# Query projection of a fused attention and feed-forward kernel: which sub-products are computed whole and which are split once more, and where two sets of token sums stand

## The chip, the cores and the metric

The kernel runs on one core of a Trainium2 chip, in one launch. The metric is the device time of that launch in microseconds (us), as the median of several runs. The engines are named as in the profile: PE (TensorE, matrix products), DVE (VectorE), ACT (ScalarE), POOL (GpSimd) and SP (SyncE, which here only issues DMAs). Each engine works through its own list of instructions in order; semaphores make one engine wait for another.

## What is computed

The reference is a cross-attention block followed by a gated feed-forward block, all in float32, on 8 sequences of 128 tokens with 512 features (1024 tokens in all), with 32 heads of 128. The lines of the attention:

```
x = _rmsnorm(hidden_states, ln_weight)
...
h_q = (x @ w_q.T).reshape(b, lq, H, DH)
h_k = (key_value_states @ w_k.T).reshape(b, lk, H, DH)
h_v = (key_value_states @ w_v.T).reshape(b, lk, H, DH)
score = jnp.einsum('bqhd,bkhd->bhqk', h_q, h_k)
score = score + position_bias[None]
...
attn = jnp.einsum('bhqk,bkhd->bqhd', score, h_v).reshape(b, lq, H * DH)
out = attn @ w_out.T
return hidden_states + out
```

The change touches the first product alone, the queries `h_q`: 1024 x 512 times 512 x 4096.

## The kernel before

**Groups.** The 32 heads are worked in 8 groups of 4 (`NG = 8`, `GH = 4`). The queries of all groups are computed first, in the loop of lines 800 to 842, and written to HBM (`store_queries`); the attention reads them back later. For group g the product is a 512 x 512 piece of the weights (`wq`) times the 512 x 1024 transposed tokens (`hT`), giving four tiles `heads[0..3]` of 128 x 1024, one for each head.

**Seven products for eight.** That product is cut into 2 x 2 blocks on each side and done by the Strassen-Winograd scheme with seven block products, numbered 1 to 7, in place of eight. It needs sums of blocks beforehand: four sums of weight blocks for each group (`combine_rows`, line 315, on POOL, 128x512 each), and four sums of token blocks once for all groups (`h_sums`). A product of the outer scheme can be computed in one of two ways:

- *whole* (`whole`, line 367): two halves of two PE matmuls with 512 columns each; ACT copies every half from PSUM to its place in `heads`.
- *split once more* by the same scheme (`inner`, line 383): seven inner products, of 128 x 256 columns each, in the order 2, 1, 5, 6, 3, 7, 4. Each inner step ends in a DVE addition that takes the PSUM bank into `heads`. Two banks alternate: inner products 2, 5 and 3 go into one, and 1, 6, 7 and 4 into the other, so a later step has to wait until DVE has taken the earlier one out of its bank. A split product needs, for each group, four 128x128 weight sums on POOL (`q_inner_rows`, line 723), and once for all groups four 128x256 sums of its token block (`inner_tokens`, line 470, four DVE instructions for each product number, all of whose inputs lie in SBUF; the third one overwrites a piece of `hT`, so the product's whole form can't be computed after it).

**Who does what.** Outer products 2, 3, 4 and 5 are always split, all four together (`inner_T`, called *quads* here): seven steps of four matmuls and three DVE additions. The quads of group g are not computed in group g but interleaved into group g+1 (the generator `quads`). Outer product 1 is whole in every group. Products 6 and 7 are whole in group 0 and single split products in groups 1 to 7 (`inner_T6` in the two banks of the pool `ps_mm`, `inner_T7` in the banks `sc` and `av` of the pool `ps`).

**Order.** During this phase all instructions of PE, DVE, ACT and POOL keep the order of the program (`InOrder`). For groups 1 to 7 it is written out by hand: first whole product 1, each half followed by one step of the quads of the group before, then line 832:

```
for k, n in enumerate((6, 6, 0, 6, 6, 0, 7, 6, 7, 6, 0, 6, 7, 7, 0, 7, 7, 0, 7)):
    next(streams[n])
    if g + 1 < NG and k in (2, 5, 8, 10):
        weigh_q(q_w[g + 1], k // 3)
    if g + 1 < NG and k == 10:
        rows_now = combine_rows(f"q{g + 1}", q_w.pop(g + 1))
```

where 0 is a step of the quads. `weigh_q` (line 707) multiplies a quarter of the next group's weights by the norm's weights, on ACT; `combine_rows` follows on POOL when all four quarters are done, and `q_inner_rows` of the next group after it.

**Token sums.** All of `inner_tokens` stands in group 0: line 819 for products 2 to 5 (16 instructions) at the third half of the whole products, line 825 for products 6 and 7 (8 instructions) at the last half. Their results lie in `q_sums` (lines 809 to 812), addressed by `q_place`.

**Room.** The 128x128 weight sums of a group lie in one of two sets of spare tiles (`row_space`, `q_rows`), groups of even and odd number by turns, taken from buffers that the attention uses later (tags `aT`, `pb`, `s4`, `p`, `pT`, `tt`). The first position bias `pb0` (line 843) is loaded into a buffer of tag `pb`.

Of the kernel before, what the change touches and what calls it, by code (L numbers as in the profile page):

```python
# [10 lines left out]
F32 = mybir.dt.float32  # L11
# [6 lines left out]
P = 128  # L18
BS = 32
# [15 lines left out]
class Later:  # L35
# [10 lines left out]
    def next(self, engine):  # L46
        if self.calls:
            op, args, kw = self.calls.pop(0)
            getattr(engine, op)(*args, **kw)
# [15 lines left out]
def xattn_ffn_kernel(  # L65
# [26 lines left out]
    NG = H // GH  # L92
# [6 lines left out]
    HW = GW // 2  # L99
    ADD, SUB = ALU.add, ALU.subtract  # L100
# [11 lines left out]
    work = pool("work", 2, side="right", reuse_waits="tile")  # L112
# [50 lines left out]
    for b in range(B):  # L163
        nc.sync.dma_start(x_in[b // 2][:, b % 2, :], x[b])

    vector, gpsimd, scalar, sync = (
        InOrder(tc, e) for e in (nc.vector, nc.gpsimd, nc.scalar, nc.sync)
    )
# [198 lines left out]
    def whole(name, product, part, count, pool=ps_mm, tag="mm"):  # L367

        m, places = {}, ((1, [(1, 1)]), (6, [(1, 2)]), (7, [(2, 2), (2, 1)]))
        for i, to in places[:count]:  # L370
            for t in range(2):
                if i == 1:
                    m[t] = pool.tile([P, 512], F32, tag=tag, name=f"mm_{name}_{t}")
                product(i, t, m[t], i == 1)
                for r, c in to:
                    scalar.copy(part(r, c, t), m[t])  # L376
                yield
# [5 lines left out]
    def inner(name, multiply, places, banks=None, fresh=False):  # L383


        one, two = banks or (
            [pl.tile([P, 2, HW], F32, tag="i", name=f"i{k}{h}_{name}") for h in range(2)]
            for k, pl in enumerate((ps_a, ps_b))
        )
        blocks = {1: (1, 1), 2: (1, 1), 3: (1, 2), 4: (2, 1), 5: (2, 2), 6: (1, 2), 7: (2, 2)}  # L390
        steps = [(i, *blocks[i]) for i in (2, 1, 5, 6, 3, 7, 4)]
        for i, r, c in steps:
            for m, (ns, place) in zip(two if i in (2, 5, 3) else one, places):
                for h, n in enumerate(ns):
                    multiply(n, i, m[:, h], i in (2, 1, 5) and h == 0)
                for to, *base, out in place(r, c, m, *((i in (2, 5, 6, 4),) if fresh else ())):
                    vector.tensor_tensor(to, *(base or [to]), out, ADD)  # L397
            yield True

    def multiply_T(a, b):  # L400
        def multiply(n, i, out, first):
            kv_tensor.matmul(out, a[n][i], b[n][i], start=first, stop=True, skip_group_check=True)  # L402

        return multiply
# [13 lines left out]
        places = ((2, 3), upper), ((4, 5), lower)  # L418
        return inner(name, multiply_T(a, b), places, fresh=fresh)

    def inner_T7(name, a, b, heads):
        def place(r, c, m, first):
            above, to = (heads[k][:, bass.ds(512 + (c - 1) * HW, HW)] for k in (r - 1, r + 1))
            return [(to, above if first else to, m[:, 0])]

        banks = [[ps.tile([P, 2, HW], F32, tag=tag, name=f"{tag}_{name}")] for tag in ("sc", "av")]
        return inner(name, multiply_T(a, b), (((7,), place),), banks, True)

    def inner_T6(name, a, b, heads):
        def place(r, c, m, first):  # L430
            left, to = (heads[r - 1][:, bass.ds(at + (c - 1) * HW, HW)] for at in (0, 512))
            return [(to, left if first else to, m[:, 0])]

        banks = [[ps_mm.tile([P, 2, HW], F32, tag="mm", name=f"m6{k}_{name}")] for k in range(2)]
        return inner(name, multiply_T(a, b), (((6,), place),), banks, True)

    def inner_V(name, a, b, pairs):
        def multiply(n, i, out, first):
# [31 lines left out]
    def inner_tokens(eng, src, half, place, products):  # L470

        blocks = {}
        for n in products:
            b = [src[n][:, c, at] for c in range(2) for at in (slice(0, half), slice(half, None))]
            b11, b12, b21, b22 = b
            t1, t2, t3, t4 = place(n)
            eng.tensor_tensor(t1, b12, b11, SUB)
            eng.tensor_tensor(t2, b22, t1, SUB)
            eng.tensor_tensor(t3, b22, b12, SUB)
            eng.tensor_tensor(t4, b21, t2, SUB)  # L480
            blocks[n] = numbered(*b, t1, t2, t3, t4)
        return blocks

    def blocks_T(name, w, src, heads):

        for j in range(GH):
            heads.append(acts.tile([P, T], F32, tag="a", name=f"{name}_{j}"))

        def product(i, t, out, first):
            for c in range(HC):  # L490
                kv_tensor.matmul(  # L491
                    out, w[i][:, c, bass.ts(t, P)], src[i][:, c, :],
                    start=(first and c == 0), stop=(c == HC - 1), skip_group_check=True,
                )

        def part(r, c, t):
            return heads[2 * (r - 1) + t][:, bass.ts(c - 1, 512)]

        return product, part
# [207 lines left out]
    def weigh_q(w, c):  # L707

        InOrder(tc, nc.scalar).mul(w[:, c], w[:, c], lnw_sb[:, c : c + 1])
# [3 lines left out]
    def spare(tag, bufs, shape=(2, 2, P)):  # L713
        return work.tile([P, *shape], F32, tag=tag, name=f"rows_{tag}", bufs=bufs)

    def row_space(tags, single):
        tiles = [spare(*t) for t in tags]
        sevens, sixes = (spare(*t, (3, P)) for t in single)
        return [t[:, k] for t in tiles for k in range(2)], {7: sevens, 6: sixes}

    q_rows = [row_space((("aT", 2), ("aT", 2), ("pb", 2)), (("s4", 1), ("p", 1)))]

    def q_inner_rows(g, w):

        pieces, single = q_rows[g % 2]
        a = {}
        for n in (6, 7) if g else ():
            quarters = [w[n][:, c, bass.ts(r, P)] for r in range(2) for c in range(2)]
            a[n] = sums_a(gpsimd, *quarters, *(single[n][:, k] for k in range(3)))
        a.update(pair_rows(w, pieces))  # L730
        return a
# [56 lines left out]
    def store_queries(g, heads):  # L788
        for j in range(GH):
            nc.sync.dma_start(queries[g][:, j, :], heads[j])  # L790
# [2 lines left out]
    kept = [dram.tile([P, 2, GW], F32, name=f"v0_kept_{i}") for i in range(B // 2)]  # L793

    def q_place(n):
        t1, t2, t4 = q_sums[3 * (n - 2) :][:3]
        return t1, t2, h_t[n][:, 0, slice(8, None)], t4

    quads, rows_now, h_inner = iter(()), rows_q, {}
    for g in range(NG):  # L800
        if g + 1 < NG:
            q_w[g + 1] = load_q(g + 1)
        else:
            kv_w[1] = load_kv(1)
        if g == 0:
            for i in range(B // 2):
                nc.sync.dma_start(kept[i], v[i])
            q_rows.append(row_space(3 * (("pT", 4),), 2 * (("tt", 2),)))
            q_sums = [
                acts.tile([P, 4, 8, BS], F32, tag="a", name=f"t_q{k}") for k in range(4)  # L810
            ] + [work.tile([P, 2, 8, BS], F32, tag="pT", name="t_q", bufs=4)]
            q_sums = [t[:, k] for t in q_sums for k in range(t.shape[1])]
        w, heads, name = rows_now, [], f"q{g}"
        tiles = whole(name, *blocks_T(name, w, h_t, heads), 1 if g else 3)
        a = q_inner_rows(g, w) if g else a_q0
        for k, _ in enumerate(tiles):
            next(quads, None)
            if g == 0 and k == 2:
                h_inner.update(inner_tokens(vector, h_t, 8, q_place, (2, 3, 4, 5)))
                vector.reciprocal(rs1, rs1)  # L820
                vector.tensor_scalar_add(res_scale, rs1, 1.0)
                vector.tensor_tensor(res_bias, mv1[:, :, 0], rs1, ALU.mult)
                vector.tensor_scalar_mul(res_bias, res_bias, -1.0)
            if g == 0 and k == 5:
                h_inner.update(inner_tokens(vector, h_t, 8, q_place, (6, 7)))
            if g == 0 and k >= 2:
                weigh_q(q_w[1], k - 2)
        if g:
            streams = {
                6: inner_T6(name, a, h_inner, heads), 7: inner_T7(name, a, h_inner, heads), 0: quads  # L830
            }
            for k, n in enumerate((6, 6, 0, 6, 6, 0, 7, 6, 7, 6, 0, 6, 7, 7, 0, 7, 7, 0, 7)):
                next(streams[n])
                if g + 1 < NG and k in (2, 5, 8, 10):
                    weigh_q(q_w[g + 1], k // 3)
                if g + 1 < NG and k == 10:
                    rows_now = combine_rows(f"q{g + 1}", q_w.pop(g + 1))
                if k == 17:
                    store_queries(g - 1, heads_before)
        if g == 0:  # L840
            rows_now = combine_rows("q1", q_w.pop(1))
        quads, heads_before = inner_T(name, a, h_inner, heads, g > 0), heads
# [719 lines left out]
```

## Time and profile before

| what | value |
|---|---|
| median of 3 runs | 1063.97 us (1063.6 to 1064.22) |
| the profiled execution: its own time | 1064.58 us |
| its span from first to last instruction | 1062.8 us |
| granted TensorE clock | 1.00 |
| POOL, DVE busy over the span | 535.3 us (50%), 751.8 us (71%) |
| query phase: first query matmul to the last | 55.4 to 230.2 us |
| group 1's first matmul | 65.7 us |
| groups 2, 3 begin | 88.20, 109.77 us |

The profile shows for each engine when it is busy. In the timeline a row is a run of equal instructions: start, length, engine, line, operation, output and inputs, shape, count, and in brackets the idle time before it and what ended it. Every float32 matmul appears as two records, so "x4" beside 128x512 is one half of a whole product (two matmuls), and "x8" beside 128x256 is one step of the quads (four matmuls); a single split step is "x2". In this phase most instructions carry line L60, which is the helper that records the order; they are told apart by their tiles: `mm_q` are banks of whole products, `m_q` banks of product 6, `sc_q` and `av_q` banks of product 7, `i_q` banks of the quads, `t_q` the token sums, `rows_...` and `S_q` the weight sums. Times are us from the start of the span.

### The profile page before, as it was taken

How to read it: one execution, taken by the hardware profiler on the slowest of the kernel's cores; microseconds unless marked ns; L12 is line 12 of the kernel's file. 1: busy time of each engine (PE TensorE's matmuls, PEld its weight loads, DVE VectorE, ACT ScalarE, POOL GpSimd, SP SyncE). 2: the span in 40 equal slices, each digit the busy share in tenths (PEclk: the TensorE clock that was granted, in tenths of full speed). 3: DMA queues.
4: the chain of work that ended last, by engine and by line, in shares of the span. 5: the costliest groups of instructions: out<-in, count | busy, mean ns of one | idle time of the engine just before them, and what ended most of it. 6: DMA issues, size and time to landing. Idle time of an engine off the chain costs nothing.

```text
span 1062.8 us, 14764 instructions
## 1 busy us (share of the span) xinstructions
PE 1052.6 (99%) x5156; PEld 845.8 (80%) x5156; DVE 751.8 (71%) x1415; ACT 305.3 (29%) x856; POOL 535.3 (50%) x583
## 2 busy tenths in 40 slices
PE   9999999999999999999999999999999999999998
PEld 5668878876888898888889769998888865667887
DVE  4697777798678778778777766774545237889852
ACT  2541112014544444444444333311000012333100
POOL 6648765808754656555552375570000336997010
PEclk9999999999999999999999999999999999999999
DMA  9543453396556554564656557774441632120011
GB/s 292 160 167 132 150 186 127 119 345 219 177 191 193 181 190 142 188 196 161 210 168 200 190 180 254 235 250 140 167 139 60 197 102 60 40 60 1 1 40 40
DMA packets 125850, 166.07 MB, mean 156 GB/s; under 512 B 15728, under 2 KB 77424, under 8 KB 125776
## 3 DMA queue, kind: packets, MB, share of 16 engines
q1 hardware_dynamic: 111360, 133.92, 38.2%
q10 hardware_dynamic: 12544, 24.38, 6.6%
q0 software_dynamic: 1872, 6.82, 2.0%
q8 instruction: 41, 0.67, 0.2%
q14 instruction: 33, 0.27, 0.1%
HBM read 106.90 MB, written 58.20 MB: 155 GB/s over the span
## 4 chain that ended last, share of the span: by engine, by line
PE 89%; DVE 5%; DMA 3%; issue 1%; ACT 1%; ACTq 0%; POOL 0%; SPq 0%; DVEq 0%; POOLq 0%
PE m L913 9%; PE i_q L60 9%; PE m L60 8%; PE mm_v L512 7%; PE mm_k L491 7%; PE i_v L440 7%; PE d L1468 6%; PE i L1333 6%; PE i_k L402 6%; PE mm_f L1373 5%; PE av L591 4%; PE sc L545 4%; PE mm_k L60 2%; PE m_q L60 2%; PE mm_q L60 2%; PE mm_v L60 2%
## 5 line engine op out<-in xcount | busy, mean ns | idle before, releaser
L60 DVE TENSOR_TENSOR q<-q,i_q 128x512 f32<-128x512 f32 x168 | 94.7, 596 | 30.9 <-PE i_q L60 27.8
L530 POOL TENSOR_TENSOR s<-pb,mneg 128x512 f32<-128x512 f32 x40 | 62.4, 1562 | 86.2 <-DVE p L569 78.0
L558 ACT ACTIVATE s<-s,nmx 128x128 f32<-128x128 f32 x240 | 93.3, 390 | 25.4 <-DVE nmx L553 18.7
L397 DVE TENSOR_TENSOR v<-v,i_v 128x512 f32<-128x512 f32 (+1 forms) x126 | 73.8, 589 | 34.7 <-PE i_v L440 23.1
L596 ACT COPY aT<-av 128x512 f32<-128x512 f32 x60 | 35.1, 585 | 168.4 <-PE av L591 130.8
L397 DVE TENSOR_TENSOR k<-k,i_k 128x512 f32<-128x512 f32 (+1 forms) x105 | 60.2, 588 | 27.6 <-PE i_k L402 26.9
L60 POOL TENSOR_TENSOR s<-pb,mneg 128x512 f32<-128x512 f32 x24 | 36.7, 1534 | 69.8 <-DVE p L60 39.0
L545 PEld LDWEIGHTS sc<-k,q 128*128 128x128 f32 x416 | 53.8, 192 | 6.6 <-issue 4.5
L545 PE MATMUL sc<-k,q 128*128 128x128 f32 x416 | 55.3, 275 | 0.0
L512 PE MATMUL mm_v<-wv,ctx_sb 128*128 128x256 f32 x224 | 52.5, 379 | 0.0
L491 PE MATMUL mm_k<-ctx_sb,wk 128*128 128x512 f32 x112 | 52.4, 593 | 0.0
L60 PE MATMUL m<-wo,a 128*128 128x256 f32 x200 | 48.5, 380 | 1.3 <-DMA a<-att 1.3
L301 DVE TENSOR_TENSOR S_a<-a 128x256 f32<-128x256 f32 x22 | 9.7, 443 | 56.3 <-DMA a<-att 43.2
L1108 POOL TENSOR_TENSOR x<-x,u 128x256 f32<-128x256 f32 x4 | 3.0, 753 | 91.8 <-DVE x L1107 91.8
L913 PE MATMUL m<-wo,a 128*128 128x256 f32 x200 | 48.4, 379 | 0.0
L591 PE MATMUL av<-pT,v 128*128 128x128 f32 x360 | 47.6, 275 | 0.0
L512 PEld LDWEIGHTS mm_v<-wv,ctx_sb 128*128 128x128 f32 x224 | 41.5, 190 | 5.0
L558 ACT ACTIVATION_READ_ACCUMULATOR s<-s,nmx 128x1 f32 x240 | 44.8, 187 | 0.0
L376 ACT COPY q<-mm_q 128x512 f32<-128x512 f32 x22 | 12.7, 586 | 110.7 <-PE mm_q L60 110.6
L569 DVE TENSOR_TENSOR p<-s,ri 128x512 f32<-128x512 f32 x52 | 43.3, 833 | 0.9
L591 PEld LDWEIGHTS av<-pT,v 128*128 128x128 f32 x360 | 43.8, 192 | 0.0
L60 PEld LDWEIGHTS m<-wo,a 128*128 128x128 f32 x200 | 37.2, 190 | 6.4 <-DMA a<-att 1.7
(433 smaller groups left out, 2742.7 us busy)
## 6 DMA issues: line engine op xcount, KB each, us to landing
queries<-q SPq DMA_DIRECT2D x32, 512.0 KB, 4.0
turned<-tt SPq DMA_DIRECT2D x64, 256.0 KB, 2.9
pT<-turned SPq DMA_DIRECT2D x64, 256.0 KB, 3.0
att<-aT ACTq DMA_DIRECT2D x64, 256.0 KB, 3.0
q<-queries SPq DMA_DIRECT2D x30, 512.0 KB, 5.1
a<-att SPq DMA_DIRECT2D x23, 512.0 KB, 4.0
wq<-in_wqT_dram SPq DMA_DIRECT2D x8, 1024.0 KB, 6.6
wk<-in_wkT_dram SPq DMA_DIRECT2D x7, 1024.0 KB, 5.6
```

The source lines that it names most:

```text
L60: return self.tc.keep_in_program_order(getattr(self.engine, op)(*args, **kw))
L397: vector.tensor_tensor(to, *(base or [to]), out, ADD)
L402: kv_tensor.matmul(out, a[n][i], b[n][i], start=first, stop=True, skip_group_check=True)
L440: kv_tensor.matmul(out[:, bass.ts(k, S)], b[n][i][:, bass.ts(k, S)], a[n][i], start=first and k == 0, stop=True, skip_group_check=True,)
L491: kv_tensor.matmul(out, w[i][:, c, bass.ts(t, P)], src[i][:, c, :], start=(first and c == 0), stop=(c == HC - 1), skip_group_check=True,)
L512: kv_tensor.matmul(out[:, bass.ts(k, HW)], src[i][:, c, bass.ts(2 * t + k, S)], w[i][:, c, :], start=(first and k == 0 and c == 0), stop=( ...
L545: tensor.matmul(sc[:, j, :], qT[:, j, bass.ts(b % 2, S)], kT[j][:, cols], start=True, stop=True)
L558: scalar.activation(s[:, j, :], s[:, j, :], AF.Exp, bias=nmx[:, j : j + 1], accum_out=sm[:, j : j + 1],)
L591: tensor.matmul(av[:, j, :], v[b // 2][:, b % 2, bass.ts(j, P)], pT[:, :, j, :], start=True, stop=True,)
L913: tensor.matmul(m[n], sa[n][:, c, :], wo_t[g][n][:, c, :], start=(g == order[0] and c == 0 and PRODUCTS.index(n) % 2 == 0), stop=(g == ord ...
L1333: nc.tensor.matmul(out, a[n][k], fine_t[n][k], start=first, stop=True, skip_group_check=True)
L1468: nc.tensor.matmul(out, lhs, rhs, start=bank not in started, stop=(i == NP - 1 or n == 8), skip_group_check=True,)
```

## The change

Three things change in the query phase.

- In groups 2 to 7 no product is whole: product 1 is split as well. Its inner steps that write a block for the first time are ACT copies (128x256), the others DVE additions. In group 1 products 1 and 6 are whole, and only 7 is a single split product. Group 0 stays as it was.
- The order is written anew: for group 1 (after the four halves of the whole products, each followed by a step of the quads) `7707707707`, for the later groups `1101160161061607676076707707`. The banks of single products now alternate between the pair in `ps_mm` and the pair `sc`, `av` from one product to the next. `weigh_q` and `combine_rows` hang on other places of the order, and `store_queries` of the group before follows after the whole order.
- The token sums of product 7 stay in group 0; those of 6 are issued in group 1 after the second step of the order, and those of 1 after the fifth. With product 1 split there are four token sums that were not there before, and four more 128x128 weight sums on POOL in each of groups 2 to 7; in group 1 four fewer. The tiles for them are taken from tags `s` and `pb`, so `pb0` is now loaded late in the query phase.

```diff
                 for to, *base, out in place(r, c, m, *((i in (2, 5, 6, 4),) if fresh else ())):
-                    vector.tensor_tensor(to, *(base or [to]), out, ADD)
+                    if base == [None]:
+                        scalar.copy(to, out)
+                    else:
+                        vector.tensor_tensor(to, *(base or [to]), out, ADD)
...
-    def inner_T7(name, a, b, heads):
...
-    def inner_T6(name, a, b, heads):
...
+    def inner_single(name, n, a, b, heads, banks):
+        def place(r, c, m, first):
+            cols = [bass.ds(at + (c - 1) * HW, HW) for at in (0, 512)]
+            corner, left = (heads[r - 1][:, at] for at in cols)
+            base, to = {
+                1: (None, corner), 6: (corner, left), 7: (left, heads[r + 1][:, cols[1]]),
+            }[n]
+            return [(to, *([base] if first else []), m[:, 0])]
+
+        return inner(f"{name}_{n}", multiply_T(a, b), (((n,), place),), banks, True)
...
-        for n in (6, 7) if g else ():
+        for n in ((), (7,), (1, 6, 7))[min(g, 2)]:
...
-        t1, t2, t4 = q_sums[3 * (n - 2) :][:3]
+        t1, t2, t4 = q_sums[3 * ((n - 2) % 7) :][:3]
...
+    ORDERS = [
+        [(int(n), k) for k, n in enumerate(order)]
+        for order in ("7707707707", "1101160161061607676076707707")
+    ]
+    bank_pairs = itertools.cycle([2 * [(ps_mm, "mm")], [(ps, "sc"), (ps, "av")]])
...
-            q_rows.append(row_space(3 * (("pT", 4),), 2 * (("tt", 2),)))
+            q_rows.append(row_space(3 * (("pT", 4),), 2 * (("tt", 2),) + (("s", 3),)))
+            q_rows[0][1][1] = spare("s", 3, (3, P))
             q_sums = [
                 acts.tile([P, 4, 8, BS], F32, tag="a", name=f"t_q{k}") for k in range(4)
-            ] + [work.tile([P, 2, 8, BS], F32, tag="pT", name="t_q", bufs=4)]
+            ] + [spare(tag, n, (2, 8, BS)) for tag, n in (("pT", 4), ("s", 3), ("pb", 2))]
...
-        tiles = whole(name, *blocks_T(name, w, h_t, heads), 1 if g else 3)
+        blocks = blocks_T(name, w, h_t, heads)
         a = q_inner_rows(g, w) if g else a_q0
-        for k, _ in enumerate(tiles):
+        for k, _ in enumerate(whole(name, *blocks, 3 - g) if g < 2 else ()):
             next(quads, None)
...
             if g == 0 and k == 5:
-                h_inner.update(inner_tokens(vector, h_t, 8, q_place, (6, 7)))
-            if g == 0 and k >= 2:
-                weigh_q(q_w[1], k - 2)
+                h_inner.update(inner_tokens(vector, h_t, 8, q_place, (7,)))
+            if k >= 2:
+                weigh_q(q_w[g + 1], k - 2)
         if g:
-            streams = {
-                6: inner_T6(name, a, h_inner, heads), 7: inner_T7(name, a, h_inner, heads), 0: quads
-            }
-            for k, n in enumerate((6, 6, 0, 6, 6, 0, 7, 6, 7, 6, 0, 6, 7, 7, 0, 7, 7, 0, 7)):
+            streams = {0: quads}
+            for n, order in ORDERS[g > 1]:
+                if n not in streams:
+                    pair = next(bank_pairs)
+                    banks = [
+                        [pl.tile([P, 2, HW], F32, tag=tag, name=f"{tag}_{name}_{n}")]
+                        for pl, tag in pair
+                    ]
+                    streams[n] = inner_single(name, n, a, h_inner, heads, banks)
                 next(streams[n])
-                if g + 1 < NG and k in (2, 5, 8, 10):
-                    weigh_q(q_w[g + 1], k // 3)
-                if g + 1 < NG and k == 10:
+                if g == 1 and order in (1, 4):
+                    h_inner.update(inner_tokens(vector, h_t, 8, q_place, (6 - 5 * (order // 4),)))
+                if g == 1 and order in (0, 3):
+                    weigh_q(q_w[2], 2 + order // 3)
+                if 1 < g < NG - 1 and order in (8, 11, 14, 17):
+                    weigh_q(q_w[g + 1], order // 3 - 2)
+                if g + 1 < NG and order == (18 if g > 1 else 4):
                     rows_now = combine_rows(f"q{g + 1}", q_w.pop(g + 1))
-                if k == 17:
-                    store_queries(g - 1, heads_before)
+            store_queries(g - 1, heads_before)
```

More of the change, by code (lines that the diff above doesn't have):

```diff
@@ L419, in inner_T @@
         return inner(name, multiply_T(a, b), places, fresh=fresh)
-    def inner_T7(name, a, b, heads):
+    def inner_single(name, n, a, b, heads, banks):
         def place(r, c, m, first):
[L423 to L427, printed above, removed]
-    def inner_T6(name, a, b, heads):
[L430 to L435, printed above, removed]
+            cols = [bass.ds(at + (c - 1) * HW, HW) for at in (0, 512)]
[5 more added lines that the diff above has]
+        return inner(f"{name}_{n}", multiply_T(a, b), (((n,), place),), banks, True)
     def inner_V(name, a, b, pairs):
@@ L717, in row_space @@
         tiles = [spare(*t) for t in tags]
-        sevens, sixes = (spare(*t, (3, P)) for t in single)
-        return [t[:, k] for t in tiles for k in range(2)], {7: sevens, 6: sixes}
+        singles = [spare(*t, (3, P)) for t in single]
+        return [t[:, k] for t in tiles for k in range(2)], dict(zip((7, 6, 1), singles))
     q_rows = [row_space((("aT", 2), ("aT", 2), ("pb", 2)), (("s4", 1), ("p", 1)))]
```

## The prediction

> **What bounds the kernel now.** First the page: how busy each engine is, and the chain that ended last.
>
> ```profile
> PE 1052.6 (99%) x5156; PEld 845.8 (80%) x5156; DVE 751.8 (71%) x1415; ACT 305.3 (29%) x856; POOL 535.3 (50%) x583
> PE 89%; DVE 5%; DMA 3%; issue 1%; ACT 1%; ACTq 0%; POOL 0%; SPq 0%; DVEq 0%; POOLq 0%
> ```
>
> PE is busy through 99% of the span: a matmul removed is a gain, a wait put before PE is a loss. Next the busy time by stretches (busy us and count for PE, PEld, DVE, ACT, POOL, then clock, DMA share, GB/s), around group 1 and in group 2:
>
> ```profile
> 72.00:92.00 20.00, 19.38 (x85) 15.72 (x84) 17.11 (x38) 2.73 (x5) 19.38 (x30) 1.00 0.26 101
> 92.00:110.00 18.00, 18.00 (x81) 15.21 (x80) 14.86 (x32) 3.15 (x5) 14.80 (x22) 1.00 0.34 124
> ```
>
> In group 1 POOL has no pause (19.38 of 20 us) and DVE little (17.11). That is the place to which the change moves work. The timeline of PE gives the unit prices:
>
> ```profile
> 75.95 1.19 PE L60 MATMUL m_q<-t_q,rows_tt 128*128 128x256 f32 x4 [0.62 <-DVE q L60]
> 87.77 0.59 PE L60 MATMUL sc_q<-t_q,wq 128*128 128x256 f32 x2
> 88.20 1.88 PE L60 MATMUL mm_q<-hT,wq 128*128 128x512 f32 x4
> 102.00 1.89 PE L60 MATMUL i_q<-hT,rows_pT 128*128 128x256 f32 x8
> 109.77 1.88 PE L60 MATMUL mm_q<-hT,wq 128*128 128x512 f32 x4
> ```
>
> Lengths overlap, so starts count: a single split step takes 87.77 to 88.20 = 0.43 us, a quads step (102.00 to 103.72) 1.73, half a whole product (88.20 to 89.92) 1.72. Groups 2 to 7 repeat every 109.77 - 88.20 = 21.57 us with no gap. Last the timelines of DVE and POOL, where token sums meet weight sums:
>
> ```profile
> 67.24 0.42 DVE L60 TENSOR_TENSOR t_q<-hT,t_q 128x256 f32<-128x256 f32 x1
> 68.03 1.38 DVE L60 TENSOR_TENSOR t_q<-hT,t_q 128x256 f32<-128x256 f32 x1
> 69.33 1.49 DVE L60 TENSOR_TENSOR hT<-hT 128x256 f32<-128x256 f32 x1
> 70.74 1.49 DVE L60 TENSOR_TENSOR t_q<-hT,t_q 128x256 f32<-128x256 f32 x1
> 78.43 1.61 DVE L60 TENSOR_TENSOR q<-q,i_q 128x512 f32<-128x512 f32 x3
> 80.29 0.41 DVE L60 TENSOR_TENSOR q<-q,m_q 128x256 f32<-128x256 f32 x1
> 80.62 0.42 DVE L60 TENSOR_TENSOR q<-q,sc_q 128x256 f32<-128x256 f32 x1
> 390.52 0.66 DVE L565 TENSOR_TENSOR ri<-sm,unseen 128x4 f32<-128x4 f32 x1
> ```
>
> ```profile
> 67.65 1.47 POOL L60 TENSOR_TENSOR S_q<-wq 128x512 f32<-128x512 f32 x1 [24.03 <-ACT wq L60]
> 69.20 1.33 POOL L60 TENSOR_TENSOR S_q<-S_q,wq 128x512 f32<-128x512 f32 x1
> 70.49 1.45 POOL L60 TENSOR_TENSOR wq<-wq 128x512 f32<-128x512 f32 x1
> 83.95 1.27 POOL L60 TENSOR_TENSOR S_q<-S_q,wq 128x512 f32<-128x512 f32 x1
> 390.39 0.76 POOL L304 TENSOR_TENSOR s_k<-S_k,s_k 128x256 f32<-128x256 f32 x1
> ```
>
> A token sum takes 0.34 us from start to start while POOL rests (66.90, 67.24, 67.58), but some 1.4 beside POOL's 128x512 sums, and each ends 0.29 us after the POOL instruction that was running (69.41 after 69.12, 70.82 after 70.53). The tiny `ri` at 390.52, also with two SBUF inputs, lasts 0.66 us and ends 0.03 after a 128x256 POOL sum; elsewhere it takes 0.15. DVE additions that read PSUM aren't affected: three for a quads step take 78.43 to 79.96 = 1.53, a single 0.33, POOL busy beside them.
>
> **Products exchanged.** A whole product costs 2 x 1.72 = 3.44 us, a single split one 7 x 0.4315 = 3.02 (0.4315 = 1.73 / 4). Groups 2 to 7: 28 + 21 matmuls x 0.4315 = 21.14 against 21.57, so -0.43 each, -2.6 together. Group 1 becomes 4 x 1.72 + 35 x 0.4315 = 22.0, 0.43 more than the pattern; but before it lasted 65.68 to 88.20 = 22.52, since it held a stall of about 0.9 (the row at 75.95 and its late matmuls), caused by the slow token sums of 67.6 to 72.2.
>
> **Cover in groups 2 to 7.** DVE: 7 x 1.53 + 17 x 0.33 = 16.3 us of 21.14; step by step every bank is out 0.4 us or more before PE wants it. POOL: 5.0 (four 128x512) + 3 x 1.78 + 5.7 = 16.1 of 21.14; the new sums of product 1 come first, some 17 us after group begin (weights weighed at 11.4, 5.0 of 128x512 sums, 0.5), and PE wants them at 21.14 + 2.6. ACT: a new copy of 128x256 has no row; it is bounded by 0 and the 0.58 of the 128x512 copy, I take 0.45. Three come early in the group while ACT idles. The fourth stands behind two `weigh_q` that wait for a DMA:
>
> ```profile
> 97.12 2.56 ACT L60 ACTIVATE wq<-wq,lnw_sb 128x512 f32<-128x512 f32 x4 [2.97 <-DMA wq<-in_wqT_dram]
> ```
>
> That is 8.9 us after group 2's begin; two of the four end at 10.2, the copy at 10.6, and product 7's second step, which takes over that bank, comes at 12.5. So 0, and as much as the DMA is later than 1.9 us if this cover goes. The late `pb0` (256 KB) arrives in group 7, some 25 us before the first scores at 233.6: 0. The stores, now behind the whole order, stand in SP's list where they stood, ahead of the next group's weights, and the tiles they free are wanted a group later: 0.
>
> **Token sums in group 1.** Unhindered, PE would run: products 1 and 6 and four quads steps, 65.68 to 79.46; then 7,7 to 80.33; quads 5 to 82.05; 7,7 to 82.92; quads 6 to 84.64; 7,7 to 85.51; quads 7 to 87.23; 7 to 87.66. DVE gets quads step 4 (begun 77.74) 1.06 us after its begin, ends it at 80.6 and two additions of 7 at 81.27; now its list has the sums of 6. POOL began at 67.65 and has done four 128x512 (5.0), four 128x128 (1.8) and eight 128x256 (5.7): it is at 80.2, waits until 80.4 for ACT, whose last three `weigh_q` now stand behind the copy of product 6 at 78.0, and starts group 2's four 128x512 sums, exactly then. The four token sums end with these, at about 86.2 (4.9 us). Queued behind: the three additions of quads step 5 (to 87.7) and two of product 7 (88.05, 88.4). PE's next step of 7 needs the first of those banks: it stands from 84.64 to 88.1, 3.5 us. Then the sums of 1, beside POOL's 128x128 sums. No row shows that pair; the bounds are 0.34 each (alone) and 1.41 (beside 128x512), and I take POOL's own 0.42 plus the 0.16 by which its 1.25 grows to 1.41: 0.58, since the 390.52 row waits out the shorter instruction and no more. 88.4 + 2.3 = 90.7. Only then quads step 6 leaves its bank, first half at 91.4; PE, ready at 89.0 for quads step 7, loses 2.4 more. Steps 7 and the last 7 end at 93.56: 5.4 us later than 88.20 before.
>
> [...]
>
> **Sum.** -2.6 + 5.4 = +2.8 us. On the profiled execution's own 1064.58 that is 1067.4; its span is 1062.8, the 1.8 around it stay. The median lies 0.61 below that execution: 1063.97 + 2.8 = **1066.8 us**. A measurement can tell 0.2%, 2.1 us: below 1061.8 is faster, above 1066.1 slower. With every token sum at 1.41 the second four take 5.6 instead of 2.3: +6.1, 1070.1.
>
> **Rivals.**
> (a) The sums cost what they do alone, 0.34, because POOL happens to wait then or DVE wins. DVE: sums of 6 to 82.6, step 5 and two to 84.8, sums of 1 to 86.2; quads 7 starts at 86.9, group 1 ends at 89.1: +0.9, with -2.6 is -1.7: 1062.3, no change that can be told. Against: POOL had 0.62 us of pause in 20.
> (b) Faster: the sums are hidden altogether. The stall before 76 us goes and DVE's additions of quads steps 5 and 6 leave the banks before PE returns: -2.6 - 0.54 (group 1: 87.66 against 88.20) = -3.1, 1060.9. It decides from the point where PE loses less than 1.0 us in all. For it: DVE has 5 us of spare time per group; against: after 79.46 it must do 3 x 1.53 + 7 x 0.33 = 6.9 us in PE's 8.2, before any sum.
> (c) Worse: the fourth ACT copy. If the weights land more than 1.9 us later than before, product 7 stands in each of groups 2 to 6; 1 us each makes +7.8, 1071.8. Against: landing came 7.9 to 8.9 us after group begin in all groups.
>
> **Chances.** Forecast 0.6, with its own range of 1065.5 to 1068.1, an error of one POOL sum (1.3 us) in where POOL stands; all sums at 1.41 0.05; (a) 0.17; (b) 0.13; (c) 0.05. Of the forecast's 0.6 some 0.13 lies below 1066.1. Slower 0.57, within 0.2% 0.30, faster 0.13. The range runs from just under (a) to all sums at 1.41, 1061.9 to 1070.1, and leaves out (b) and (c).
>
> **What would show it.** Right: in the changed profile the sums of 6 (`hT<-hT` and its three neighbours) near 81 to 86 us, 1.2 to 1.5 us each beside `S_q` on POOL; those of 1 near 0.6; two waits of PE on DVE of about 3.5 and 2.4 us; group 2 beginning near 93.6; then a period of 21.14 without gaps. Wrong: sums of 0.42, no wait of PE there, a period other than 21.14, or PE waiting for ACT at product 7.

## The result and the profile after

| | before | after |
|---|---|---|
| median | 1063.78 us (1063.56 to 1064.22, 4 runs) | 1069.05 us (1068.5 to 1070.21, 4 runs) |
| ratio to before, 95% interval | | 1.005 [1.0033, 1.0068] |
| the profiled execution: its own time, its span | 1064.58, 1062.8 us | 1069.48, 1067.7 us |
| group 2 begins; first matmul of the next phase (`mm_k`) | 88.20; 230.18 us | 95.63; 235.14 us |

The changed kernel is slower by about 5.3 us, as forecast in sign, and 2.25 us above the forecast of 1066.8. The page, its busy times and the shares of the chain that ended last:

```profile
PE 1053.9 (99%) x5186; PEld 853.5 (80%) x5186; DVE 759.9 (71%) x1430; ACT 308.3 (29%) x870; POOL 543.5 (51%) x603
PE 89%; DVE 5%; DMA 3%; ACT 1%; issue 1%; POOL 0%; ACTq 0%; SPq 0%; DVEq 0%; POOLq 0%
```

Read alone, this page misleads: PE is busy for 1.3 us more than before (1052.6) although the change takes work away from it in six groups (seven matmuls of 256 columns in place of four of 512, so the count of records rises by 30). The time by stretches says why. Its columns are busy us and count for PE, PEld, DVE, ACT and POOL, then the granted clock, DMA share and GB/s:

```profile
84.00:88.40 4.40, 1.02 (x5) 0.57 (x4) 4.40 (x7) 0.00 (x0) 4.32 (x7) 1.00 0.00 0
88.80:95.20 6.40, 5.34 (x13) 3.78 (x12) 4.78 (x10) 0.00 (x0) 6.24 (x11) 0.50 0.36 144
95.60:97.00 1.40, 1.40 (x8) 1.22 (x8) 1.21 (x4) 0.37 (x1) 1.32 (x3) 1.00 0.17 70
```

At the end of group 1 PE stands for most of 4.4 us; afterwards it is granted **half its clock**, from about 88.6 to 95.4 us, and matmuls that take twice as long count as busy. The timeline of PE, with the idle time before a row and what ended it in brackets (in this kernel the `mm_q` rows of 128x256 in group 1 are steps of product 7, and those of `av_q` and `mm_q` that begin groups 2 and 3 are steps of product 1):

```profile
84.43 0.59 PE L60 MATMUL i_q<-hT,S_q 128*128 128x256 f32 x2
88.43 1.04 PE L60 MATMUL mm_q<-hT,rows_tt 128*128 128x256 f32 x2 [3.40 <-DVE q L60]
91.39 1.22 PE L60 MATMUL i_q<-t_q,wq 128*128 128x256 f32 x2 [1.06 <-DVE q L60]
92.40 1.06 PE L60 MATMUL i_q<-t_q,S_q 128*128 128x256 f32 x2
93.25 1.06 PE L60 MATMUL i_q<-t_q,wq 128*128 128x256 f32 x2
95.63 0.59 PE L60 MATMUL av_q<-hT,wq 128*128 128x256 f32 x2
116.78 1.03 PE L60 MATMUL mm_q<-hT,wq 128*128 128x256 f32 x4
```

Both predicted waits are there, each for DVE: 3.40 and 1.06 us. The 128x256 rows behind the first one last 1.04 to 1.22 us in place of 0.59; from start to start it is 0.85 (92.40 to 93.25) in place of 0.43. Group 2 begins at 95.63, group 3 at 116.78: a period of 21.15. DVE and POOL in the same stretch:

```profile
81.67 0.54 DVE L60 TENSOR_TENSOR t_q<-hT 128x256 f32<-128x256 f32 x1
82.25 1.37 DVE L60 TENSOR_TENSOR t_q<-hT,t_q 128x256 f32<-128x256 f32 x1
83.54 1.48 DVE L60 TENSOR_TENSOR hT<-hT 128x256 f32<-128x256 f32 x1
84.95 1.48 DVE L60 TENSOR_TENSOR t_q<-hT,t_q 128x256 f32<-128x256 f32 x1
86.35 1.60 DVE L60 TENSOR_TENSOR q<-q,i_q 128x512 f32<-128x512 f32 x3
88.53 0.41 DVE L60 TENSOR_TENSOR rows_s<-hT 128x256 f32<-128x256 f32 x1
89.47 0.67 DVE L60 TENSOR_TENSOR hT<-hT 128x256 f32<-128x256 f32 x1
90.66 1.60 DVE L60 TENSOR_TENSOR q<-q,i_q 128x512 f32<-128x512 f32 x3
```

```profile
80.66 1.27 POOL L60 TENSOR_TENSOR S_q<-wq 128x512 f32<-128x512 f32 x1 [0.21 <-ACT wq L60]
83.30 1.44 POOL L60 TENSOR_TENSOR wq<-wq 128x512 f32<-128x512 f32 x1
84.71 1.44 POOL L60 TENSOR_TENSOR S_q<-wq,S_q 128x512 f32<-128x512 f32 x1
89.22 0.63 POOL L60 TENSOR_TENSOR S_q<-S_q 128x128 f32<-128x128 f32 x1
```

The four sums of product 6 take 81.67 to 86.35, 4.68 us, in step with POOL's 128x512 sums; the four of product 1 (the rows `rows_s<-hT` and `hT<-hT`; their results lie in spare tiles with the names of weight sums) take 88.53 to 90.66, 2.13 us, and POOL's 128x128 sums beside them last 0.63 in place of 0.45.

### The profile page after: what moved, and what is told of

The parts are those of the page before. It is cut to its first block, busy times and chain, and to the rows that moved or that the text cites. A ratio compares the mean times of both kernels' runs of the same rounds, so it can differ in the third digit from the quotient of the medians.

```text
span 1067.7 us, 14878 instructions
## 1 busy us (share of the span) xinstructions
PE 1053.9 (99%) x5186; PEld 853.5 (80%) x5186; DVE 759.9 (71%) x1430; ACT 308.3 (29%) x870; POOL 543.5 (51%) x603
## 4 chain that ended last, share of the span: by engine, by line
PE 89%; DVE 5%; DMA 3%; ACT 1%; issue 1%; POOL 0%; ACTq 0%; SPq 0%; DVEq 0%; POOLq 0%
PE m L925 9%; PE i_q L60 9%; PE m L60 7%; PE mm_v L510 7%; PE mm_k L489 7%; PE i_v L438 7%; PE d L1480 6%; PE i L1345 6%; PE i_k L405 6%; PE mm_f L1385 5%; PE mm_q L60 4%; PE av L589 4%; PE sc L543 4%; PE mm_k L60 2%; PE mm_v L60 2%; PE sc_q L60 1%
## 5 line engine op out<-in xcount | busy, mean ns | idle before, releaser
L547 DVE TENSOR_TENSOR s<-sc,s 128x512 f32<-128x512 f32 x52 | 35.3, 680 | 9.4 <-PE sc L543 9.4
```

## The experiments

All were timed in five rounds beside the kernel before (medians 1063.64 in the first set of four, 1063.70 in the second set of three). The diffs are against the changed kernel.

**1. No sums of 6 and 1.** Are the token sums the whole loss? The kernel leaves them out: without an engine `inner_tokens` issues nothing, and POOL fills their tiles with zeros early.

```diff
-                    h_inner.update(inner_tokens(vector, h_t, 8, q_place, (6 - 5 * (order // 4),)))
+                    h_inner.update(inner_tokens(None, h_t, 8, q_place, (6 - 5 * (order // 4),)))
...
+            for k in (12, 13, 14, 18, 19, 20):
+                gpsimd.memset(q_sums[k], 0.0)
```

> The changed kernel without the eight token sums of products 6 and 1 (they are left out of the computation; their tiles are zeroed early by POOL, while it rests). Theory: the whole loss hangs on these sums, so PE has no wait in group 1, group 2 begins 22.0 us after group 1 (29.7 in the changed kernel), the clock stays at 1.00, and the time is about 3.1 us below the kernel before, near 1060.7 us. Rival, that something else of the change costs time (the new banks, the ACT copies, the other order): PE still waits in groups 1 to 7, and the time stays above 1063.

Measured: 1061.04 us (1059.73 to 1061.97, 11 runs), ratio 0.9975 [0.9966, 0.9983]. The timeline of PE has no wait in this phase, and group 2 begins 7.86 us earlier than in the changed kernel:

```profile
87.77 0.59 PE L60 MATMUL av_q<-hT,wq 128*128 128x256 f32 x2
```

All of the loss hangs on the eight sums; without them the change brings 2.6 us.

**2. POOL rests beside the sums.** The order of DVE stays, but POOL, before it starts group 2's weight sums, reads one column of the last result of product 1's sums.

```diff
+                if g == 1 and order == 4:
+                    rest = small.tile([P, 1], F32, tag="rest", name="rest", bufs=1)
+                    gpsimd.tensor_scalar_add(rest, q_sums[20][:, 0, :1], 0.0)
```

> All eight sums in place on DVE, but a tiny POOL instruction that reads the last of them stands ahead of group 2's weight sums, so POOL rests while DVE does them. Theory, that the sums are slow because they wait out POOL's instructions: each takes 0.34 us from start to start, PE waits once, about 1.4 us, in group 1 and perhaps 0.4 us for POOL's late sums in group 2, and the time is about 1.5 us below the kernel before, near 1062.3. Rival, that eight more DVE instructions in a row are too much whatever POOL does: the waits of 3.4 and 1.1 us stay and the time is near 1069.

Measured: 1063.79 us (1062.71 to 1065.93, 11 runs), ratio 1.0005 [0.9996, 1.0014]. The timelines of DVE and of PE:

```profile
82.28 0.43 DVE L60 TENSOR_TENSOR t_q<-hT,t_q 128x256 f32<-128x256 f32 x1
82.62 0.42 DVE L60 TENSOR_TENSOR hT<-hT 128x256 f32<-128x256 f32 x1
```

```profile
85.38 0.67 PE L60 MATMUL mm_q<-hT,rows_tt 128*128 128x256 f32 x2 [0.20 <-DVE q L60]
87.69 0.70 PE L60 MATMUL i_q<-t_q,wq 128*128 128x256 f32 x2 [1.20 <-DVE q L60]
90.02 0.59 PE L60 MATMUL av_q<-hT,wq 128*128 128x256 f32 x2
```

The sums start 0.34 us apart, 0.42 each, on the same engine behind the same instructions: POOL's sums beside them are what made them 1.4 (product 6) and up to 0.6 (product 1). The time missed the expectation by 1.5 us. Even at 0.34 the sums make PE wait. Group 2 begins 2.25 us later than in experiment 1, of which 0.26 was there before the sums (the row `i_q<-hT,S_q` ahead of the first wait starts at 84.58, not 84.32): 2.0 instead of the 1.4 of the working. POOL's pause also makes the weight sums late in group 2 by 0.26 us. The remaining 0.5 of the 2.75 us between the two medians has no single place in the traces.

**3. PE kept busy in the waits.** Seven useless 128x256 products in front of the step that waits 3.4 us and four in front of the step that waits 1.06; each is 0.43 us, so they fit into the waits.

```diff
+                if g == 1 and order in (5, 7):
+                    idle = ps.tile([P, 2, HW], F32, tag="sc", name=f"idle_{order}")
+                    for _ in range(7 if order == 5 else 4):
+                        kv_tensor.matmul(idle[:, 0], ident, q_sums[0], start=True, stop=True)
```

> The changed kernel, with 7 and 4 matmuls without a use (128x256, into a bank that is free in group 1) put where PE waits for DVE, ahead of product 7's sixth and of the last quads step. DVE's list is the same, so the waits stay as they are. Theory, that PE's clock is halved after the wait of 3.4 us and that this is the part of the loss which the prediction lacked: granted clock 1.00 throughout, group 2 begins near 93.6 instead of 95.6, time near 1066.9. Rival, that PE was slow after the wait for another cause (operands late, DVE): group 2 begins at 95.6 again and the time stays near 1069.

Measured: 1067.39 us (1066.06 to 1067.97, 5 runs), ratio 1.0037 [1.0024, 1.0049]. The timeline of PE:

```profile
84.81 3.19 PE L60 MATMUL idle<-t_q,ident 128*128 128x256 f32 x14
88.39 0.67 PE L60 MATMUL mm_q<-hT,rows_tt 128*128 128x256 f32 x2 [0.39 <-DVE q L60]
89.33 1.89 PE L60 MATMUL idle<-t_q,ident 128*128 128x256 f32 x8
93.68 0.59 PE L60 MATMUL av_q<-hT,wq 128*128 128x256 f32 x2
```

The useful step still starts at 88.39, so DVE is as late as before; the granted clock is 1.00 throughout, and group 2 begins at 93.68, 1.95 earlier. **Eleven matmuls more make the kernel shorter.** This start is what the prediction had (93.56). The two medians are 1.66 us apart, and the intervals of the two ratios overlap; but all five times lie below all four of the changed kernel, and the clock and the start of group 2 say the same.

**4. The sums on POOL.** Sums of 1 and 6 move from DVE to POOL, after the second and the fourth half of group 1's whole products; group 1's 128x256 weight sums, wanted only in group 2, go behind group 2's 128x512 sums and product 1's.

```diff
+            if g == 1 and k == 1:
+                h_inner.update(inner_tokens(gpsimd, h_t, 8, q_place, (1,)))
+            if g == 1 and k >= 2:
+                for c in (2 * k - 4, 2 * k - 3):
+                    weigh_q(q_w[2], c)
+            if g == 1 and k == 3:
+                h_inner.update(inner_tokens(gpsimd, h_t, 8, q_place, (6,)))
+                rows_now = combine_rows("q2", q_w.pop(2))
+                ones = single_rows(2, rows_now, 1)
+                a.update(pair_rows(w, q_rows[1][0]))
...
-                if g == 1 and order in (1, 4):
-                    h_inner.update(inner_tokens(vector, h_t, 8, q_place, (6 - 5 * (order // 4),)))
```

> The same eight sums on POOL: those of 1 right after the whole product 1 of group 1, those of 6 after the whole product 6, and the 128x256 weight sums of group 1, which nobody wants before the third quads step of group 2, moved behind group 2's 128x512 sums and product 1's rows. Theory: each sum takes POOL 0.7 us, it is never late, DVE has no more to do than in groups 2 to 7, no wait of PE in the query phase; time near 1060.8, faster than both kernels by 3 and 8 us. Rival, that POOL is full in groups 1 and 2 and its rows come late: PE waits for POOL at the start of group 2 by 1 us or more, time 1062 to 1066.

Measured: 1060.94 us (1059.94 to 1062.09, 11 runs), ratio 0.9976 [0.9967, 0.9985]. POOL, then PE:

```profile
74.69 0.72 POOL L60 TENSOR_TENSOR rows_s<-hT 128x256 f32<-128x256 f32 x1
79.72 0.72 POOL L60 TENSOR_TENSOR t_q<-hT,t_q 128x256 f32<-128x256 f32 x1
80.41 1.26 POOL L60 TENSOR_TENSOR S_q<-wq 128x512 f32<-128x512 f32 x1
```

```profile
87.88 0.59 PE L60 MATMUL av_q<-hT,wq 128*128 128x256 f32 x2
```

Eight sums of 0.72 us cost POOL 5.7 us, taken from work with a later due time; PE never waits in this phase. The time is that of the kernel without the sums, 2.7 us below the kernel before: this version beats both.

**5 and 6. One set of sums alone.** Experiment 1 with the sums of 6 left out and those of 1 kept, and the other way round; each leaves its four sums out and fills their tiles with zeros.

```diff
-                    h_inner.update(inner_tokens(vector, h_t, 8, q_place, (6 - 5 * (order // 4),)))
+                    eng = None if order == 1 else vector
+                    h_inner.update(inner_tokens(eng, h_t, 8, q_place, (6 - 5 * (order // 4),)))
```

> VectorE's four token sums of product 6 are left out (their three tiles are zeroed early by GpSimd, so that part of the output is not the reference's); the four of product 1 stay. The 3.4 us wait must go. By the ledger product 1's sums come forward beside the rest of the second group's 128x512 weight sums on GpSimd, so the first of them cost more than 0.6 us each; TensorE waits some 1 to 2 us before step 7 of the quads, its clock stays at full speed, the second group begins about 90.0 (2.2 us later than with both sets left out), and the time is about 1063.2 us. The rival, that each set costs about half of what the two cost together: about 1065.0 us.

> VectorE's four token sums of product 1 are left out (their three tiles are zeroed early by GpSimd, so that part of the output is not the reference's); the four of product 6 stay. Clock theory: the 3.4 us wait at 85 stays, the granted clock is halved for some 7 us behind it, the second wait goes but was short there anyway, the second group begins about 94.4 and the time is about 1067.8 us. The rival, in which the clock does not matter and only the waits count: the second group begins about 91.5 and the time is about 1064.9 us.

Measured with the sums of 1 alone: 1064.13 us (1062.56 to 1065.53, 11 runs), ratio 1.0003 [0.9994, 1.0011]. PE's timeline and the time by stretches:

```profile
88.08 0.70 PE L60 MATMUL i_q<-t_q,wq 128*128 128x256 f32 x2 [2.16 <-DVE q L60]
91.73 0.96 PE L60 MATMUL av_q<-hT,wq 128*128 128x256 f32 x2
```

```profile
88.40:88.80 0.40, 0.40 (x3) 0.37 (x2) 0.40 (x2) 0.00 (x0) 0.32 (x2) 1.00 0.00 0
89.20:92.40 3.20, 3.20 (x9) 2.54 (x9) 2.30 (x6) 0.00 (x0) 3.11 (x7) 0.50 0.00 0
92.80:96.00 3.20, 3.20 (x17) 2.81 (x16) 2.13 (x4) 0.92 (x3) 3.12 (x5) 1.00 0.97 331
```

The wait is 2.16 us where 1 to 2 was expected, and it too halves the clock in this execution, from about 89.1 to 92.5, 3.4 us that start 1.0 us after PE resumed. The eleven executions fall into two kinds by their mean granted clock: six at 0.998 with a median of 1064.6 us, five at 0.999 or 1.0 with 1063.2, the number expected at full clock. Half the clock for 3.4 of 1063 us is 0.0016 of the mean, and by this count costs 1.7 us; the two medians differ by 1.4. Only the first of the eleven has a trace: that the other five at 0.998 lost their clock at this place is inferred from the mean.

Measured with the sums of 6 alone: 1066.34 us (1065.47 to 1067.51, 8 runs), ratio 1.0027 [1.0016, 1.0037], between the two theories. PE's timeline and one stretch:

```profile
89.78 0.67 PE L60 MATMUL mm_q<-hT,rows_tt 128*128 128x256 f32 x2 [3.40 <-DVE q L60]
92.94 0.59 PE L60 MATMUL av_q<-hT,wq 128*128 128x256 f32 x2
```

```profile
89.60:96.00 6.40, 6.22 (x29) 5.30 (x30) 5.84 (x14) 0.37 (x1) 6.17 (x13) 1.00 0.69 275
```

The same 3.40 us pause, and here the clock **stays** at 1.00. (This execution runs 1.35 us late from a wait in the first keys: the row before the pause starts at 85.78, not 84.43. Less that, group 2 begins at 91.6, the rival's 91.5.) But it was the only one of the eight at 1.0: six had a mean clock of 0.998, one 0.996. Neither theory holds as it was put: the clock does matter, but a pause of 3.4 us does not always halve it, and where it does it is, as far as the mean clocks tell, mostly for one stretch of 3.4 us and not for two.

**7. Two useless products only.** As experiment 3 with two products in the first wait and none in the second, so that PE pauses for about 2.5 us.

> Two useless 128x256 matmuls (0.43 us each) at the start of the first wait alone, so that TensorE's pause is about 2.5 us instead of 3.4; nothing else differs from the changed kernel. If only a pause of about 3.4 us halves the clock: granted clock 1.00 behind it, second wait about 2 us, time about 1067 us as with the waits filled. If a pause of 2.5 us halves it too: clock about 0.5 for some 7 us behind it and about 1069 us. If the clock falls in some executions and not in others, the times spread between the two.

Measured: 1068.85 us (1067.9 to 1069.31, 5 runs), ratio 1.0046 [1.0034, 1.0059]. PE's timeline and the time by stretches:

```profile
88.56 0.67 PE L60 MATMUL mm_q<-hT,rows_tt 128*128 128x256 f32 x2 [2.54 <-DVE q L60]
91.52 1.22 PE L60 MATMUL i_q<-t_q,wq 128*128 128x256 f32 x2 [1.86 <-DVE q L60]
```

```profile
89.60:90.80 1.20, 0.06 (x1) 0.00 (x0) 1.20 (x4) 0.00 (x0) 1.20 (x3) 1.00 1.00 410
91.20:94.40 3.20, 2.88 (x7) 2.35 (x8) 2.54 (x6) 0.00 (x0) 3.07 (x6) 0.50 0.01 1
94.80:98.00 3.20, 3.20 (x16) 2.83 (x15) 2.46 (x5) 0.37 (x1) 3.12 (x5) 1.00 0.46 183
```

After the 2.54 us pause the clock was full; it fell at about 91.0, inside the second, shorter pause, and came back at 94.4, again after 3.4 us. All five executions had a mean of 0.996 to 0.998. So two matmuls weren't enough, and the length of a single pause isn't the rule: 2.54 us here and 3.40 us in experiment 6 left the clock full in the trace, 2.16 us in experiment 5 did not.

## Why the prediction was right, and by what it fell short

**The exchange in six groups: right.** -2.6 us was predicted for groups 2 to 7; the period is 21.15 us against the 21.14 of the working. With the stall of group 1 gone as well, the working had -3.1; with the sums left out (experiment 1) the medians differ by -2.6 and the first `mm_k` starts 2.9 earlier (227.28).

**Cover: right.** No wait of PE for ACT, POOL or a DMA shows in groups 2 to 7. The new ACT copies take 0.37 us where 0.45 was taken. `pb0` and the stores cost nothing that shows.

**Prices of the sums: right.** Four sums of 6 at 4.68 us (4.9 predicted), four of 1 at 2.13 (2.3); experiment 2 shows that POOL sets them (0.34 us from start to start while POOL rests), experiments 1 and 4 that nothing else stands behind the loss. Both sides get longer beside each other: a sum of product 6 lasts 1.48 us where it takes 0.42 alone, POOL's 128x512 sum 1.44 where it takes 1.27. From start to start a token sum takes 1.41 us beside a 128x512 sum, and 0.60 beside a 128x128 one in the last rows of product 1. Why the two lengthen each other's instructions, no run shows.

**PE's first wait: right,** 3.40 us against 3.5.

**What fell short is the price of that wait.** The prediction charged PE for the time it stands and let it resume at full speed ("PE stands from 84.64 to 88.1", then "loses 2.4 more", "steps 7 and the last 7 end at 93.56"). In fact PE ran at half clock for 6.8 us behind the first wait. Part of that loss is hidden in the second wait, which is 1.06 here and 1.86 in experiment 7, where the clock was full ahead of it; the rest put group 2 at 95.63. So the term of the sum that was too small is group 1's: 5.4 us were worked out, and from 88.20 to 95.63 it is 7.43. Some 0.2 of the difference is there before group 1 begins (its first step of the quads starts at 67.62 in this execution, at 67.40 before); the clock is most of the rest, for experiment 3 removes its share alone and lands at 93.68. The measured 1069.05 lies 0.95 above the forecast's own range and 1.05 below the rival in which every sum takes 1.41, but that rival's reason did not occur: the sums of product 1 took 0.45 to 0.60.

By medians, from no sums to the changed kernel:

| step | from, to | us |
|---|---|---|
| the sums at their own 0.34, and POOL's pause | 1061.04 to 1063.79 | 2.75 |
| POOL's weight sums beside them | 1063.79 to 1067.39 | 3.60 |
| the clock behind the waits | 1067.39 to 1069.05 | 1.66 |

The last row compares two sets of runs, whose medians of the kernel before differ by 0.14.

**The rivals.** (a) had the right mechanism for a resting POOL but was too cheap: 1062.3 against 1063.79 in experiment 2. The loss before step 7 of the quads was right (from 85.89 to 87.69, less the 0.43 of a step, 1.37 against 1.4); not in the working were 0.37 us lost in the same way before 85.38 and POOL's late weight sums. (b) is what the change would be with the sums out of the way: 1060.9 worked out, 1060.94 in experiment 4, whose runs of before lay 0.3 lower. (c), the late ACT copy, did not occur.

**What halves the clock.** Shown: filling the pauses keeps it full (five of five executions at 1.0); pauses of 0.20 and 1.20 us left it at 0.999 or 1.0 in all eleven executions; pauses of 2.16 us and more halve it, as far as the mean clocks tell, in six of eleven executions (experiment 5), seven of eight (6), all five (7) and all four (changed kernel); the halved stretches are 3.4 us (experiments 5 and 7) or 6.8 us (changed kernel), and begin 0.2 us (changed kernel) or 1.0 us (experiment 5) after PE has resumed, or within a later pause (experiment 7). The stretch of 6.8 us held the pause of 1.06 us; those of 3.4 us held none (experiment 5) and the last 0.5 us of the second pause (experiment 7). One execution of each kernel has a trace; for the others only the mean clock speaks.

Not shown: what decides. No run tells why a pause of 3.40 us was followed by half clock in the changed kernel and by none in the trace of experiment 6, or why the half clock ended when it did. A pause of 1.20 us never halved it (experiment 2), one of 2.16 us did, by the mean clocks, in six of eleven executions (experiment 5); what lies between stays open.

## What to carry to other kernels

Before you put two-input SBUF instructions on VectorE, look at what GpSimd does at that very moment: here instructions of 0.34 us took up to 1.4, and with eight of them TensorE ran dry (waits of 3.40 and 1.06 us), while the same sums on GpSimd, ahead of work that is wanted later, cost nothing that the time shows. Waits of TensorE of 2.16 us and more had a second price here, in six of eleven executions or more by the mean clocks: half clock in or behind them, for 3.4 to 6.8 us in the traces that show it. Read the granted clock in fine stretches behind each wait, and count matmuls that run at half clock as lost time although the page calls them busy. When pauses can't be avoided, cheap filler matmuls can pay (eleven of them in pauses of 3.40 and 1.06 us brought 1.7 us), but a partial fill of two did not (1068.85 us against 1069.05).

## What was not expected of the hardware

A pause of 3.40 us was followed by half clock for 6.8 us in one trace (changed kernel) and by none in another (experiment 6), with the same matmuls ahead of it. And the slowing beside POOL reaches down to small instructions: a 128x256 DVE sum beside POOL's 128x128 sums took 0.60 us from start to start in place of 0.34, and stretched those from 0.45 to 0.63.
